# Two of every four blocks of attention probabilities turned by VectorE and a round trip through DRAM, with keys stored in strips

## The chip, the cores and the metric

The kernel runs on one NeuronCore of a Trainium2 chip. The number that counts is the device time of one execution in microseconds. The kernel before took 1162.42 us (median of three runs, 1162.05 to 1164.58). The core has a matrix engine (TensorE; PE in the profile, with PEld for the loads of its stationary operand), a vector engine (VectorE; DVE), an activation engine (ScalarE; ACT), GpSimd (POOL) and SyncE (SP), whose queue issues every DMA of this kernel. All data are float32.

## The reference, cut to what matters

```python
x = x + layernorm(attention(layernorm(x)))   # x: 4 sequences of 512 tokens, 1024 wide
x = x + layernorm(ffn(layernorm(x)))

# attention: 32 query heads of width 32, 8 key/value heads, rotary positions
scores = einsum('bhqd,bhkd->bhqk', q, k) / sqrt(32)
scores = where(causal, scores, -1e20)
attn   = softmax(scores, axis=-1)
out    = einsum('bhqk,bhkd->bhqd', attn, v)  # then @ w_o.T + b_o

# ffn: x @ base_w.T + base_b + 2 * LoRA mixture of the 2 best of 8 experts
```

Softmax runs over the keys. The product with v sums over keys too, so on TensorE the keys of the probabilities must lie on the partitions, while the scores come out with the queries on the partitions. The probabilities therefore have to be transposed between the two.

## The kernel before, in words

**Tiles.** The 2048 tokens are 16 tiles of 128, four to a sequence; tile i of a sequence (i = 0 to 3) attends to i + 1 key blocks of 128. The dense products (q, w_o and the base matrix of the ffn) are done for pairs of token tiles with a seven-product scheme (`seven`, L655). Each of their weight blocks, a "piece" of 128 x 512 (256 KB), is read from DRAM for one use, through a ring of `RING` = 13 buffers (`bring_pieces`, L476; issue at L489). The products are issued at L618. The key and value weights stay in SBUF.

**A group.** Attention goes by groups (`Group`, L1371). A group is one token tile and n = 4, 2, 1, 1 columns of heads for i = 0, 1, 2, 3; a column holds four heads, one in each 32-partition strip, and these four are the "quadrants" r. A group has m = n (i + 1) = 4, 4, 3, 4 key blocks in each quadrant. `scores` (L1382) issues the score products into the one PSUM tile `sc`; VectorE adds the causal mask and takes the maxima (L1459, L1469); ScalarE takes the exponentials into a tile `pr` for each quadrant and sums them (L1411); VectorE inverts the sums (L1440); GpSimd multiplies `pr` by them (L1425). `turn` (L1480), once for each quadrant, transposes the m blocks of `pr` on TensorE (L1485) into a PSUM bank, which is copied to a tile `prT` (`copy`, L331, on ScalarE or VectorE). `values` (L1498) then issues the products with v (L1508), and its result is copied to `aT`, the input of the w_o product. `pr` and `prT` share the `SOFT` = 8 buffers of one pool.

**The order of the work** is not left to the engines. `Order` (L92) runs through the whole program in advance with written durations, and emits each engine's instructions in the order that results; an engine then executes its own list strictly in that order and waits where data are not there. Some of its durations: a DMA occupies SP's queue for its kilobytes divided by `RATE` = 370 and is taken to have landed `LANDS` = 2.8 us later; a dense product takes 0.858 us; a hand-over between engines 0.1 us (`SIGNAL`).

TensorE's steps stand in lanes: scores; urgent transposes of activations; a value lane, which holds in turn the four turns of a group, its values step, the turns of the next group, and so on; and the dense lanes. `_choice` (L202) takes the first lane in that order that has been ready for `SAFE` = 0.3 us. A values step is put last while the next scores step "comes", that is while everything the scores need apart from the exponentials before them has been planned; and in the kernel before a scores step is put last while the values step comes but is not ready. If the values step is ready when scores are issued, both go out together (`tensor`, L236), with one switch of TensorE into its 32-row or 32-column tiling. The scores of group k also need the turns of group k - 2.

**SP.** Every DMA stands in SP's one list: pieces, x tiles (`load_x`, `load_y`), results, and in the first 240 us the sums and differences of weight blocks that the seven-product scheme needs, which `mix` (L409) computes and writes to DRAM. A DMA that has to wait for a semaphore keeps everything behind it in the list waiting.

Of the kernel before, what the change touches and what calls it, by code (L numbers as in the profile page):

```python
# [16 lines left out]
P = 128  # L17
# [5 lines left out]
MASKED = -1e30  # L23
QUADS = P // HD


# [65 lines left out]
class Order:  # L92
# [109 lines left out]
    def _choice(self, scores, values, lanes):  # L202
# [7 lines left out]
        if score is not None and value is not None:  # L210
            if self._comes(score):
                waiting.append(values)
            if self._comes(value) and not self._is_ready(value):
                waiting.append(scores)
        for lane in lanes:
# [50 lines left out]
def kernel(  # L266
# [26 lines left out]
    QSCALE = 1.0 / math.sqrt(HD)  # L293
    BANKS, SOFT, RING = 4, 8, 13

# [5 lines left out]
    kvpool = ctx.enter_context(tc.tile_pool(name="kvpool", bufs=4))  # L301
    soft = ctx.enter_context(tc.tile_pool(name="soft", bufs=SOFT))
    weights = ctx.enter_context(tc.tile_pool(name="weights", bufs=RING))
    small = ctx.enter_context(tc.tile_pool(name="small", bufs=2))
# [6 lines left out]
    banks = Slots(BANKS)  # L311
    soft_slots, part_slots, piece_slots = Slots(SOFT), Slots(4), Slots(RING)
    xnT_slots, aT_slots, hT_slots = Slots(2), Slots(3), Slots(2)
    qT_slots, kT_slots, raw_slots, turn_slots = Slots(8), Slots(4), Slots(6), Slots(1)
    xa_slots, y_slots, w_slots, v_slots = Slots(1), Slots(3), Slots(4), Slots(8)
    order = Order(banks)
# [14 lines left out]
    def copy(n, out, in_):  # L331

        return Op(
            0,
            act=(0.15 + n * 0.00085, lambda: nc.scalar.copy(out(), in_())),  # L335
            dve=(0.15 + n * 0.00105, lambda: nc.vector.tensor_copy(out(), in_())),  # L336
        )
# [9 lines left out]


    ident = const.tile([P, P], F32, name="ident")
    make_identity(nc, ident)  # L350
    cmask = const.tile([P, P], F32, name="cmask")
    make_causal_mask(nc, cmask, MASKED)

# [141 lines left out]
    class Norm:  # L495
# [60 lines left out]
        def apply(self, dst, src, h):  # L556
            cols = slice(h * 512, (h + 1) * 512)
            yield Op(
                self.urgent,
                dve=(  # L560
                    0.66,
                    lambda: nc.vector.tensor_scalar(
                        dst()[:, cols], src()[:, cols], self.rstd, self.shift, ALU.mult, ALU.add
                    ),
                ),
                act=(
                    0.82,
                    lambda: nc.scalar.activation(  # L568
                        dst()[:, cols], src()[:, cols], AF.Identity, bias=self.shift, scale=self.rstd
                    ),  # L570
                ),
            )
# [299 lines left out]
    def load_y(tok):  # L872

        yield y_slots.take()
        yield has_rest if tok in pairs[0] else all_mixed

        def issue():
            tok.y = xpool.tile([P, D], F32, tag="y", bufs=3, name=f"y_{tok.t}")
            nc.sync.dma_start(out=tok.y, in_=x[tok.t * P : (tok.t + 1) * P, :])

        yield sp(P * D * 4 / 1024 / RATE, issue)
        yield LANDS
        tok.has_y.finish(order.at)
# [33 lines left out]
    def keys_values(job):  # L917
# [38 lines left out]
        def turn_k():  # L956
# [4 lines left out]
            def end():  # L961
                yield step_k.done
                raw_slots.give(order.at)
                for kt in range(NKT):
                    yield copy(
                        P,
                        lambda: seq.k_tile(kt)[:, i * P : (i + 1) * P],
                        lambda: pt[:, kt, :],
                    )
# [401 lines left out]
    class Group:  # L1371
        def __init__(self, tok, at, n):
# [6 lines left out]
            self.pr, self.prT = [None] * QUADS, [None] * QUADS  # L1379
            self.has_prT = [Task() for _ in range(QUADS)]  # L1380

    def scores(g):  # L1382
# [19 lines left out]
        def quadrant(r):  # L1402
            urgent = 1 + r / QUADS
            yield soft_slots.take()
            pr = soft.tile([P, GROUP, P], F32, tag="soft", name=f"pr_{g.name}_{r}")
            pr = g.pr[r] = pr.rearrange("p a b -> p (a b)")
            for c in range(g.n):
# [3 lines left out]
                    lambda: nc.scalar.activation(  # L1411
                        pr[:, c * n : (c + 1) * n],
                        sc4[:, r, c, :],
                        AF.Exp,
# [6 lines left out]
            for c in range(g.n):  # L1421
# [3 lines left out]
                    lambda: nc.gpsimd.tensor_scalar(  # L1425
                        pr[:, c * n : (c + 1) * n],
                        pr[:, c * n : (c + 1) * n],
                        rtot[:, r, c : c + 1],
# [48 lines left out]
        for h in range(QUADS // 2):  # L1477
            start(totals(h), order.now)

    def turn(g, r):  # L1480
# [17 lines left out]
    def values(g):  # L1498
# [5 lines left out]
        for c in range(g.n):  # L1504
            for j in range(i + 1):
                for r in range(QUADS):
# [3 lines left out]
                        lhsT=g.seq.v[j][:, head * HD : (head + 1) * HD],  # L1510
                        rhs=g.prT[r][:, c * (i + 1) + j, :],
                        start=(j == 0),
# [3 lines left out]
        def end():  # L1516
            yield g.valued.done
            for r in range(QUADS):
                soft_slots.give(order.at)
            yield copy(  # L1520
                g.n * P, lambda: tok.aT[:, g.at : g.at + g.n, :], lambda: av[:, : g.n, :]
# [84 lines left out]
    for k, g in enumerate(groups):  # L1606
# [4 lines left out]
        if k > 1:  # L1611
# [4 lines left out]
            Step(0.109 * blocks, partial(turn, g, r), [g.normed[r | 1]], bank=True, turns=True)  # L1616
            for r in range(QUADS)
        ]
# [135 lines left out]
```

## Time and profile before

| | before |
|---|---|
| median of three runs | 1162.42 us |
| profiled execution: its time, its span | 1164.45 us, 1162.7 us |
| mean granted TensorE clock | 0.996 |
| DVE, ACT, POOL busy | 832.6, 530.1, 611.7 us |
| DMA queue of SP: bytes, busy share of 16 DMA engines | 230.12 MB, 60.7% |
| transposes of probabilities on PE (L1485) | 1280, weight loads 144.5 us busy |
| copies of `prT` on ACT, on DVE | 261 for 134.1 us, 91 for 58.3 us |
| normalisation of `pr` on POOL (L1425) | 512 for 300.5 us |

A row of the profile's groups gives the line, the engine, the operation, output and inputs, their shapes, how often it ran, the busy time and the mean duration, and what the engine waited for. A dense product and a score product each appear as two records. PE records overlap, so PE's time for a step is better read from the distance of one start to the next than from the durations. The queue of SP is written SPq.

### The profile page before, as it was taken

What the parts mean: (1) busy time and instruction counts of PE and PEld (TensorE: products, weight loads), DVE (VectorE), ACT (ScalarE), POOL (GpSimd) and SP (SyncE); (2) the same over time, 40 slices, a digit from 0 to 9 for tenths busy, and PEclk for the clock granted to TensorE, in tenths of its full rate; (3) what the DMA queues carried; (4) which work ended last, traced back from release to release, by engine and by line L of the source; (5) the groups of instructions that cost most, each with busy time, mean ns of one, the idle gap of its engine ahead of it and who ended that gap; (6) DMA issues with size and microseconds to landing.
All of it is one profiled execution on the core that took longest, in us unless ns stands there. A gap on an engine that the chain in (4) does not pass through costs nothing.

```text
span 1162.7 us, 21371 instructions
## 1 busy us (share of the span) xinstructions
PE 1136.4 (98%) x7240; PEld 624.5 (54%) x7240; DVE 832.6 (72%) x1629; ACT 530.1 (46%) x1545; POOL 611.7 (53%) x859
## 2 busy tenths in 40 slices
PE   7999999999999999999999999999999999999997
PEld 3455554655556455565555555456555555556443
DVE  4787767987678756787667876768866787668564
ACT  0354554555555355555434434455644555454010
POOL 2686856743756435544555253654545564547231
PEclk9999999999999999999999999999999999999999
DMA  9879777563773637625477443673457745585783
GB/s 349 277 255 310 248 253 263 170 220 97 257 239 96 199 109 253 192 83 176 141 244 256 137 135 118 219 229 106 149 168 233 243 135 160 164 268 187 221 285 118
DMA packets 117740, 231.48 MB, mean 199 GB/s; under 512 B 13440, under 2 KB 14464, under 8 KB 117632
## 3 DMA queue, kind: packets, MB, share of 16 engines
q1 hardware_dynamic: 117632, 230.12, 60.7%
q8 instruction: 58, 0.95, 0.3%
q14 instruction: 50, 0.41, 0.1%
HBM read 209.09 MB, written 20.97 MB: 198 GB/s over the span
## 4 chain that ended last, share of the span: by engine, by line
PE 86%; DVE 7%; DMA 3%; POOL 1%; ACT 1%; issue 1%; SPq 0%; POOLq 0%; ACTq 0%
PE acc_f L618 18%; PE acc_o L618 16%; PE acc_q L618 14%; PE pt_p L1485 11%; PE acc_kv L618 8%; PE sc L1390 7%; PE av L1508 6%; PE acc_gl L618 2%; DVE nmax L1469 2%; PE pt_xn L593 1%; PE pt_h L593 1%; DMA piece<-in_w_qkv_dram 1%; ACT pr L1411 1%; PE pt_q L1010 1%; DMA xa<-in_x_dram 1%
## 5 line engine op out<-in xcount | busy, mean ns | idle before, releaser
L1425 POOL TENSOR_SCALAR pr<-pr,rtot 128x256 f32<-128x256 f32 (+3 forms) x512 | 300.5, 602 | 251.9 <-DVE rtot L1440 183.3
L1411 ACT ACTIVATE pr<-sc,nmax 128x256 f32<-128x256 f32 (+3 forms) x512 | 265.0, 536 | 121.8 <-DVE nmax L1469 63.6
L1469 DVE TENSOR_REDUCE nmax<-sc 128x2 f32<-128x768 f32 (+3 forms) x176 | 198.2, 1126 | 33.7 <-ACT pr L1411 30.6
L1485 PEld LDWEIGHTS pt_p<-ident,pr 128*128 128x128 f32 x1280 | 144.5, 141 | 59.3 <-issue 49.1
L1485 PE MATMUL pt_p<-ident,pr 128*128 128x128 f32 x1280 | 173.2, 276 | 2.4 <-DVE raw_q L727 1.0
L335 ACT COPY prT<-pt_p 128x512 f32<-128x512 f32 (+1 forms) x261 | 134.1, 548 | 62.4 <-PE pt_p L1485 61.0
L1459 DVE TENSOR_TENSOR sc<-sc,cmask 128x256 f32<-128x256 f32 (+2 forms) x176 | 96.7, 550 | 48.6 <-PE sc L1390 39.0
L335 ACT COPY aT<-av 128x128 f32<-128x128 f32 (+2 forms) x83 | 26.1, 315 | 222.1 <-PE av L1508 222.0
L618 PE MATMUL acc_f<-piece,s_f 128*128 128x512 f32 x256 | 120.1, 602 | 2.1 <-DVE s_f L343 2.1
L618 PE MATMUL acc_kv<-wkv_sb,T_xn 128*128 128x512 f32 x256 | 119.4, 597 | 0.0
L1411 ACT ACTIVATION_READ_ACCUMULATOR pr<-sc,nmax 128x1 f32 x512 | 108.3, 212 | 0.0
L618 PE MATMUL acc_o<-piece,aT 128*128 128x512 f32 x232 | 105.9, 594 | 0.0
L618 PE MATMUL acc_q<-piece,s_q 128*128 128x512 f32 x224 | 105.4, 595 | 0.1
L618 PE MATMUL acc_q<-piece,T_xn 128*128 128x512 f32 x224 | 103.9, 594 | 0.1
L618 PE MATMUL acc_o<-piece,s_o 128*128 128x512 f32 x224 | 102.8, 593 | 0.0
L1390 PE MATMUL sc<-kT,qT 32*128 32x384 f32 (+3 forms) x1024 | 93.9, 464 | 0.5 <-ACT pr L1411 0.5
L1508 PEld LDWEIGHTS av<-prT,v 128*32 128x32 f32 x2560 | 64.8, 109 | 50.1 <-issue 35.0
L618 PE MATMUL acc_f<-piece,T_h 128*128 128x512 f32 x192 | 90.0, 592 | 0.0
L343 POOL TENSOR_TENSOR y<-y,w 128x512 f32<-128x512 f32 x61 | 79.1, 1309 | 20.3 <-ACT w L568 14.9
L1508 PE MATMUL av<-prT,v 128*32 128x128 f32 x2560 | 88.7, 276 | 0.2 <-DVE prT L336 0.2
L336 DVE COPY prT<-pt_p 128x512 f32<-128x512 f32 (+1 forms) x91 | 58.3, 642 | 31.3 <-PE pt_p L1485 29.7
L541 POOL TENSOR_TENSOR rstd<-veps,neg_half 128x1 f32<-128x1 f32 x64 | 35.0, 549 | 86.1 <-DVE veps L537 85.8
(154 smaller groups left out, 1416.3 us busy)
## 6 DMA issues: line engine op xcount, KB each, us to landing
piece<-mixed_f SPq DMA_DIRECT2D x128, 256.0 KB, 3.5
piece<-in_w_o_dram SPq DMA_DIRECT2D x116, 256.0 KB, 3.6
piece<-mixed_q SPq DMA_DIRECT2D x112, 256.0 KB, 3.4
piece<-mixed_o SPq DMA_DIRECT2D x112, 256.0 KB, 4.1
piece<-in_w_qkv_dram SPq DMA_DIRECT2D x100, 256.0 KB, 3.7
piece<-in_w_base_dram SPq DMA_DIRECT2D x96, 256.0 KB, 3.3
xa<-in_x_dram SPq DMA_DIRECT2D x32, 256.0 KB, 3.8
y<-in_x_dram SPq DMA_DIRECT2D x16, 512.0 KB, 5.7
```

Source lines behind the costliest of these rows:

```text
L335: act=(0.15 + n * 0.00085, lambda: nc.scalar.copy(out(), in_())),
L336: dve=(0.15 + n * 0.00105, lambda: nc.vector.tensor_copy(out(), in_())),
L343: engine.tensor_tensor(out=out(), in0=in0(), in1=in1(), op=op)
L541: nc.gpsimd.tensor_tensor(out=self.rstd, in0=self.veps, in1=neg_half, op=ALU.pow)
L618: nc.tensor.matmul(acc[0][:, :n], lhsT=lhsT(c), rhs=w(c), start=(c == 0), stop=last)
L1390: nc.tensor.matmul(sc[:, r, c * n : (c + 1) * n], lhsT=tok.qT[g.kt][rows, (g.at + c) % GROUP, :], rhs=seq.kT[g.kt][rows, :n], start=True, ...
L1411: lambda: nc.scalar.activation(pr[:, c * n : (c + 1) * n], sc4[:, r, c, :], AF.Exp, bias=nmax[:, r, c : c + 1], accum_out=total[:, r, c : ...
L1425: lambda: nc.gpsimd.tensor_scalar(pr[:, c * n : (c + 1) * n], pr[:, c * n : (c + 1) * n], rtot[:, r, c : c + 1], 1.0, ALU.mult, ALU.mult,),
L1459: lambda: nc.vector.tensor_tensor(out=diag, in0=diag, in1=cmask.unsqueeze(1).unsqueeze(1).to_broadcast([P, q, g.n, P]), op=ALU.add,),
L1469: lambda: nc.vector.tensor_reduce(nmax[:, some, : g.n], sc4[:, some], AX.X, ALU.max, negate=True),
L1485: nc.tensor.transpose(pt[:, j, :], g.pr[r][:, j * P : (j + 1) * P], ident)
L1508: nc.tensor.matmul(av[r * HD : (r + 1) * HD, c, :], lhsT=g.seq.v[j][:, head * HD : (head + 1) * HD], rhs=g.prT[r][:, c * (i + 1) + j, :], ...
```

## The change

Quadrants 0 and 1 of each group (r < `TURNED` = 2) are turned as before. Quadrants 2 and 3 go another way, in the new function `flip`: VectorE transposes each 32 x 32 square of the two quadrants' probabilities in place with one instruction (1024 elements a partition where m = 4, 768 where m = 3); a DMA writes the tile to a DRAM tile `there`; a second DMA, which waits for the first to land, reads it back into a tile `flat`, with rows placed so that the whole blocks come out transposed. The first moves 4 KB runs (3 KB where m = 3), the second 1 KB runs (768 B). The values products read `flat` in four runs of 32 elements.

For this the keys inside each block of 128 are held in another order: the copies to `kT` and the causal mask put key 4k + s at place 32s + k. The exponentials of quadrants 0 and 1 are written back in the original order (steps of four elements); those of quadrants 2 and 3 go into the tile `pair`, by strips.

Room and order change with it: `pair` and `flat` have two buffers each of 4 KB a partition; `SOFT` goes from 8 to 7, `RING` from 13 to 8, the y tiles from three to two. `copy` and `Norm.apply` run on ScalarE alone, where they could also go to VectorE. `_choice` no longer puts a scores step last while the values step is not ready. `Order` plans the rest around this.

```diff
-            if self._comes(value) and not self._is_ready(value):
-                waiting.append(scores)
...
-    BANKS, SOFT, RING = 4, 8, 13
+    BANKS, SOFT, RING = 4, 7, 8
+    PAIRS, FLATS = 2, 2
+    SIDE = 32
+    NS = P // SIDE
...
-    xa_slots, y_slots, w_slots, v_slots = Slots(1), Slots(3), Slots(4), Slots(8)
+    xa_slots, y_slots, w_slots, v_slots = Slots(1), Slots(2), Slots(4), Slots(8)
...
             act=(0.15 + n * 0.00085, lambda: nc.scalar.copy(out(), in_())),
-            dve=(0.15 + n * 0.00105, lambda: nc.vector.tensor_copy(out(), in_())),
...
+    def strips_of(a):
+        return a.rearrange("p (s k) -> p s k", s=NS)
+    def by_strip(a):
+        return a.rearrange("p (k s) -> p s k", s=NS)
...
-                        lambda: seq.k_tile(kt)[:, i * P : (i + 1) * P],
-                        lambda: pt[:, kt, :],
+                        lambda: strips_of(seq.k_tile(kt)[:, i * P : (i + 1) * P]),
+                        lambda: by_strip(pt[:, kt, :]),
...
+    def flip(g):
+        m = g.n * (g.tok.i + 1)
+        q = QUADS - TURNED
+        yield pair_slots.take()
+        g.pair = flips.tile([P, NS, q, m, SIDE], F32, tag="pair", bufs=PAIRS, name=f"pair_{g.name}")
+        g.has_pair.finish(order.at)
+        yield g.normed[TURNED:]
+        flat_pair = g.pair.rearrange("p s r m k -> p (s r m k)")
+        yield dve(
+            0.1 + NS * q * m * SIDE * 0.00105,
+            1,
+            lambda: nc.vector.transpose(out=flat_pair, in_=flat_pair),
+        )
+        there = dram.tile([NS, P, q * m * SIDE], F32, tag="there", bufs=4, name=f"there_{g.name}")
+        us = P * NS * q * m * SIDE * 4 / 1024 / RATE
+        yield sp(us, lambda: nc.sync.dma_start(
+            out=there.rearrange("a (k s) r -> (a k) (s r)", s=NS), in_=flat_pair), -1)
+        yield LANDS
+        pair_slots.give(order.at)
+        yield flat_slots.take()
+        g.flat = flips.tile([P, NS, q, m, SIDE], F32, tag="flat", bufs=FLATS, name=f"flat_{g.name}")
+        yield sp(us, lambda: nc.sync.dma_start(
+            out=g.flat.rearrange("p a r m q -> p a (r m q)"), in_=there.rearrange("a p r -> p a r")), -1)
+        yield LANDS
+        for r in range(TURNED, QUADS):
+            g.has_prT[r].finish(order.at)
...
-                        rhs=g.prT[r][:, c * (i + 1) + j, :],
+                        rhs=(
+                            g.prT[r][:, c * (i + 1) + j, :]
+                            if r < TURNED
+                            else g.flat[:, :, r - TURNED, c * (i + 1) + j, :]
+                        ),
...
             Step(0.109 * blocks, partial(turn, g, r), [g.normed[r | 1]], bank=True, turns=True)
-            for r in range(QUADS)
+            for r in range(TURNED)
```

## The prediction

> **What bounds the kernel now.** I read the page's busy time first, then the chain that ended last.
>
> ```profile
> PE 1136.4 (98%) x7240; PEld 624.5 (54%) x7240; DVE 832.6 (72%) x1629; ACT 530.1 (46%) x1545; POOL 611.7 (53%) x859
> ...
> PE 86%; DVE 7%; DMA 3%; POOL 1%; ACT 1%; issue 1%; SPq 0%; POOLq 0%; ACTq 0%
> PE acc_f L618 18%; PE acc_o L618 16%; PE acc_q L618 14%; PE pt_p L1485 11%; PE acc_kv L618 8%; PE sc L1390 7%; PE av L1508 6%; PE acc_gl L618 2%; DVE nmax L1469 2%; PE pt_xn L593 1%; PE pt_h L593 1%; DMA piece<-in_w_qkv_dram 1%; ACT pr L1411 1%; PE pt_q L1010 1%; DMA xa<-in_x_dram 1%
> ```
>
> TensorE is the bound: 86% of the chain is its work, and the list of waits gives PE itself some 18 us in all, 7.3 of them before its first instruction. So work taken from PE is worth its full length only while nothing new makes PE wait. The transposes are 11% of the chain.
>
> Next I read the order of time in a stretch of i = 3 (start, duration, engine; the bracket is idle time).
>
> ```profile
> 449.79 0.31 PEld L1390 LDWEIGHTS sc<-kT,qT 32*128 32x128 f32 x8 [0.76 <-issue]
> 449.79 1.14 PE L1390 MATMUL sc<-kT,qT 32*128 32x512 f32 x8
> 450.86 0.86 PE L1508 MATMUL av<-prT,v 128*32 128x128 f32 x24
> ...
> 457.03 3.12 POOL L1425 TENSOR_SCALAR pr<-pr,rtot 128x512 f32<-128x512 f32 x4 [3.06 <-DVE rtot L1440]
> ...
> 459.13 1.14 PE L1390 MATMUL sc<-kT,qT 32*128 32x512 f32 x8
> ...
> 460.20 0.86 PE L1508 MATMUL av<-prT,v 128*32 128x128 f32 x24
> 460.99 1.09 PE L1485 MATMUL pt_p<-ident,pr 128*128 128x128 f32 x8
> ```
>
> Groups follow each other every 9.1 to 9.3 us (sc at 440.67, 449.79, 459.13). A group's probabilities are normalised 10.4 us after its scores began (457.03 + 3.12 = 460.15). Each values step (av) leaves directly behind scores of a later group, so it waits for its partner and has slack.
>
> Last, the DMA rows (KB each, median us from issue to landing) and SP's own waits.
>
> ```profile
> piece<-mixed_q SPq DMA_DIRECT2D x112, 256.0 KB, 3.4
> y<-in_x_dram SPq DMA_DIRECT2D x16, 512.0 KB, 5.7
> mixed_q<-mix_q SPq DMA_DIRECT2D x8, 512.0 KB, 7.3
> mixed_f<-mix_f SPq DMA_DIRECT2D x8, 512.0 KB, 4.4
> ...
> SPq L489 <- DMA mixed_q<-mix_q: 27.3, 4, 7.5
> ```
>
> A 512 KB transfer lands after 4.4 to 7.3 us. The last line: four times SP stood before a piece because that piece reads what an earlier DMA was still writing, up to 7.5 us, with all other DMAs behind it.
>
> **The change, part by part.** The sum is made on the span, 1162.7 us; the profiled run took 1164.45, the median is 1162.42, so a span counts as a time here.
>
> *Transposes removed.* 640 of 1280. 11.3% of the chain for 1280 is 131.4 us, 0.103 each (8 from 460.99 take 0.82 us to the next load: the same). **-65.7 us.**
>
> *Pairing lost.* Scores entered with 0.76 us idle on the weight loader against the usual 0.24: 0.52 us for the switch of tiling; av behind them adds about 0.2. A values step that goes alone pays 0.52 in place of 0.2. By the argument below about two in three of 88 groups (176 reductions at L1469, two a group) go alone: 59 x 0.32 = **+19 us**; 0 to 28.
>
> *The new way to `flat`.* 56 groups have 512 KB in each direction, 32 have 384 KB: 41.9 MB out and 41.9 MB back. The plan gives it, after normalising: VectorE 1.18 + 0.1, then twice 1.38 on SP + 0.1 + 2.8, 9.8 us in all, so values at 10.4 + 9.8 = 20.2 us after the scores. Two periods are 18.5, so scores k+2 have gone, and scores k+3 do not "come", because they need the turns of k+1, which stand behind values k in the lane. So values k are planned the moment that they are ready, plus 0.3 (SAFE) and half a dense step (0.43): 0.7 us of slack. On the chip: 1.22 (nearest VectorE row, the 1024-element maximum) + 5.7 + 5.7 (the y row) = 12.6 us, 2.8 later than planned. PE executes in the planned order and waits, and behind values k stand the turns, the next scores and all dense work. Between scores k and values k lie the waits of three values steps, so each is (2.8 - 0.7)/3 = 0.7 us: 88 x 0.7 = **+62 us**. Bounds: nothing if the plan leaves 2.1 us more; with 7.3 out and 7.1 back (wgl, 544 KB in 544 B runs), (5.8 - 0.7)/3 x 88 = 150. I take y because its load state is that of most of the run.
>
> Here a rule speaks for the change: the Trainium skill, "DMA: Bandwidth & Descriptors", section "Anatomy of one DMA", fits 2.0 us + bytes/436 GB/s to a transfer (by the GpSimd path), 3.2 us for 512 KB. By it both legs take 6.4 us, less than the planned 8.6, and this term is zero: 1148 us in all. The rows of this trace say 4.4 to 7.3, so I keep the row.
>
> *SP's list.* The first leg waits for VectorE, the second for the first to land; behind both stand pieces, x tiles and results. The second leg is planned 4.3 us after the first and lands at 5.7: SP is blocked 1.4 us a group. What hid a late piece was the ring: 13 x 0.86 = 11.2 us of dense work, now 8 x 0.86 = 6.9, less 3.5 to land: 3.4 us. One block fits, one together with a y tile and two legs in the queue does not. Between 0 and 1.4 us a group; I take 0.25, near the end where the ring covers it: **+22 us**; upper bound 123.
>
> *The first 200 us.* Shares of the DMA engines in 29 us windows there: 0.97, 0.82, 0.73, 0.92, 0.72, 0.79, 0.79, with 15 groups (30 maxima). About 15 MB more at 400 GB/s, which the best short slices reached, is 38 us; idle is 18% of 203 = 36 us. It just fills: 0 to 40, I take **+10 us**.
>
> *What I cost at nothing.* VectorE loses copies (91.1 us) and normalisations (38.7) and gains 56 x 1.22 + 32 x 0.96 = 99 us. ScalarE: 530 - 134 (`prT` now) + 97 (176 copies at 0.587 or 0.482) + 29 (other copies) + 47 (58 at 0.811) = 569 us, 49%: hidden by PE, but every copy out of PSUM now queues behind exponentials, which come 4 in 3.6 us, and four banks wait for it. Strided forms have no row: exponentials of quadrants 0 and 1, GpSimd's multiply by strips, `kT`, values reading four runs. From 0 to twice their time, the first two would add up to 1.5 us a group to the chain to `flat`, the last up to 36 us to PE; I take 0, the row of the plain form. `SOFT` 7 and two y tiles: at most 6 probability tiles are held at once; 0.
>
> **Sum:** 1162.7 - 65.7 + 19 + 62 + 22 + 10 = **1210 us**.
>
> A rule against the change: "TensorE: Matmul & The Clock Gate", section "The HAM clock gate", halves PE's clock after an idle window of about 3.4 us. This trace shows it already near the end (PE busy, its loads, the others; then clock, DMA share, GB/s):
>
> ```profile
> 1128.77 5.40 PE L618 MATMUL acc_f<-piece,s_f 128*128 128x512 f32 x8 [2.10 <-DVE s_f L343]
> ...
> 1130.00:1132.00 2.00, 2.00 (x4) 0.81 (x3) 1.69 (x10) 0.00 (x0) 0.13 (x1) 0.55 0.40 130
> 1132.00:1134.00 2.00, 2.00 (x4) 0.73 (x3) 0.19 (x1) 0.00 (x0) 0.00 (x0) 0.60 0.57 145
> ```
>
> 2.1 us of idle brought the clock to 0.55, and 8 records took 5.2 us in place of 3.4: a wait of 2 us costs nearly 4. By the rule alone waits of 0.7 us are free of it, by the row waits from about 2 us are not; so the sum has none, and the upper case has it.
>
> **Rivals.** (1) *The transit is covered, and it gets faster.* Two quadrants need only be there by values; if the plan holds values k for the scores of k+2 or k+3, 2.1 us more are free and only pairing, SP and start remain: 1162.7 - 65.7 + 19 + 10 = 1126, down to 1107 if pairs stay. It decides as long as values wait under 0.5 us a group (47/88). For it: no wait of PE today, and periods of 13 us on average (1162/88). Against: 9.2 us where i is 2 or 3, and 5.7 us for 512 KB. Chance 0.18. (2) *DMA becomes the bound.* 230 MB keep the engines busy 706 us; 84 MB more at the same 326 GB/s add 257, with short runs at half speed in the second leg up to 400: 963 to 1110 us, and windows that stand at 0.78 with three groups would need 1.1 to 1.3. Legs then land after 7 to 9 us, pieces miss the ring of 8, PE waits over 2 us and its clock falls: 1.5 us a group at SP in place of 0.25 gives 1320; I give it 1250 to 1340. Against: slices of 400 GB/s exist. Chance 0.23. (3) *Gain and waits cancel* within 0.2% (2.3 us, about what a measurement of this kernel can tell): 0.03.
>
> **How the numbers follow.** The likeliest case, waits for `flat` larger than the transposes saved, has 0.56, and a range of its own of 1165 to 1250. The range 1125 to 1300 leaves out the deeper part of (1) and the upper part of (2), about 0.09 each. Faster is (1), 0.18; same 0.03; slower 0.79.
>
> **What would show it.** The trace after should have 640 transposes; waits of PE or PEld at L1508 for DMA `flat` of 40 to 100 us; SPq waiting for DMA `there` in most groups; legs landing at 5 to 7 us; waits for pieces above today's 3 us a line; av mostly not directly behind sc. I am wrong if values wait for nothing (then rival 1), or if waits for pieces exceed those for `flat` (rival 2).

## The result, and the profile after

The changed kernel took **1221.62 us** (median, 1218.12 to 1224.64), beside 1163.12 us for the kernel before on the same chip: a ratio of **1.050**, 95% interval 1.047 to 1.053. The profiled execution took 1221.72 us, its span is 1220.0, 57.3 more than before.

The page's busy times, the granted clock in 40 slices, and the DMA queue's row:

```profile
PE 1118.3 (92%) x6600; PEld 568.3 (47%) x6600; DVE 804.3 (66%) x1491; ACT 600.0 (49%) x1581; POOL 627.0 (51%) x874
...
PEclk9998889999899999999999999999999999989969
...
q1 hardware_dynamic: 176768, 314.01, 76.2%
```

The 640 transposes are gone (6600 records for 7240), yet PE is busy only 18.1 us less, and it idles 101.7 us (1220.0 - 1118.3) where it idled 26.3. The clock row shows one cause: it dips in the slices from 91 to 183 us, at 305 us and near the end; the mean is 0.971, before 0.996.

The page's groups that answer to the change's parts (busy, mean ns of one, idle before):

```profile
L1432 ACT ACTIVATE pr<-sc,nmax 128x128 f32<-128x128 f32 (+3 forms) x256 | 202.9, 844 | 265.8 <-DVE sc L1480 143.2
...
L1570 PE MATMUL av<-flat,v 128*32 128x128 f32 x1280 | 90.5, 283 | 23.6 <-DMA flat<-there 23.5
...
L1547 PE MATMUL pt_p<-ident,pr 128*128 128x128 f32 x640 | 99.6, 291 | 12.2 <-ACT aT L340 7.7
L1432 ACT ACTIVATE pair<-sc,nmax 128x128 f32<-128x128 f32 (+3 forms) x256 | 133.5, 541 | 2.8 <-issue 1.8
L1515 DVE STREAM_TRANSPOSE pair<-pair 128x1024 f32<-128x1024 f32 (+1 forms) x88 | 100.2, 1139 | 10.4 <-POOL pair L1446 10.1
...
L1570 PE MATMUL av<-prT,v 128*32 128x128 f32 x1280 | 93.5, 282 | 0.3 <-DVE w L733 0.3
```

Values that read `flat` in four runs take 283 ns, those that read `prT` 282: the strided read is free. Exponentials that are written back in the original order (`pr`) take 844 ns in the mean, those written by strips (`pair`) 541: that form is not.

The DMA rows (KB each, median us from issue to landing), then two rows of PE's waits and three of SP's (us in all, times, longest):

```profile
piece<-mixed_f SPq DMA_DIRECT2D x128, 256.0 KB, 4.3
...
there<-pair SPq DMA_DIRECT2D x56, 512.0 KB, 3.7
piece<-mixed_q SPq DMA_DIRECT2D x112, 256.0 KB, 4.4
flat<-there SPq DMA_DIRECT2D x56, 512.0 KB, 4.9
```

```profile
PE av L1570 <- DMA flat<-there: 23.5, 14, 4.9
PE pt_h L599 <- ACT w L574: 13.8, 2, 10.1
```

```profile
SPq L1522 <- DVE pair L1515: 123.0, 57, 7.4
SPq L1533 <- DMA there<-pair: 102.3, 69, 5.1
...
SPq L885 <- DMA out_dram<-y: 15.6, 12, 2.4
```

The two transfers land after 3.7 and 4.9 us, together 8.6, just what the plan gives them (2 x 4.3). PE waits for `flat` only 14 times (its weight loads 20 times, for 28.9 us). SP stands 102 us before second transfers and 123 us before first ones that wait for their squares. Pieces land after 4.4 us where it was 3.4 (`mixed_q`).

The long `pt_h` wait is in the last tiles. The timeline there (start, duration, engine; the bracket is idle time):

```profile
1169.38 0.45 SPq L1308 DMA_DIRECT2D out_dram<-y  x1
...
1173.49 0.33 SPq L885 DMA_DIRECT2D y<-in_x_dram  x1
...
1177.18 1.26 POOL L347 TENSOR_TENSOR y<-y,w 128x512 f32<-128x512 f32 x1 [3.85 <-DMA y<-in_x_dram]
...
1182.63 1.97 PE L599 MATMUL pt_h<-ident,w 128*128 128x128 f32 x8 [10.14 <-ACT w L574]
```

A y tile is loaded only after the result of an earlier token tile has been stored out of the same buffer; the sum, the norm and PE's transposes stand behind it, and PE idles 10 us.

**Where the 57 us lie.** PE idle: +75.4. PE busy: -18.1.

Of the added idle time, 23.5 us are waits for `flat` and 13 the longer waits at `pt_h`. The other 39 are many short ones, mostly for ScalarE and VectorE: 7.7 us at `pt_p` for the copies to `aT` (none before), 15.6 before the transposes of keys and queries (4.2 before), 5.7 at scores for the exponentials into `pair` (0.5 before).

The busy time holds three parts. The 640 transposes at 0.103 us are -65.7. The switches into a 32-wide tiling rise from 102 to 163 in PE's timeline; a stretch of the changed kernel shows what one costs:

```profile
123.82 5.31 PE L624 MATMUL acc_q<-piece,s_q 128*128 128x512 f32 x12
129.06 0.93 PE L1398 MATMUL sc<-kT,qT 32*128 32x384 f32 x8
129.92 1.99 PE L624 MATMUL acc_q<-piece,s_q 128*128 128x512 f32 x4
131.74 1.88 PE L624 MATMUL acc_q<-piece,T_xn 128*128 128x512 f32 x4
133.55 0.30 PE L1570 MATMUL av<-prT,v 128*32 128x128 f32 x2
```

Dense records start 0.43 us apart. The twelve before the scores take 5.24 us, 0.09 more than 12 x 0.43; the four behind them 1.82, 0.10 more; the four before the values step again 0.09 more. Two steps that go out together enter and leave the tiling once in place of twice, so 61 more switches are about +12 us (61 x 0.2).

The clock is the third part. The granted clock is 0.50 in 70 us of the changed kernel, and PE is busy in 48.6 of them (3.4 before). Half of the difference is +23 us; the mean clock, 1220 x 0.029 less 1162.7 x 0.004, gives 31, of which 8 fall where PE has nothing to do. The three parts give -31. Of the 13 us that are missing, some 9 can be the ends of records before a wait, by estimate: PE waits 76 times in place of 20, and a dense record lasts 0.59 us where the next one would start after 0.43. The rest is unexplained.

**A second reading, of the written order.** `Order` writes the lists with its own durations, so the kernel's code, with `Order` run by itself, also says when it believes that SP's last instruction ends. That is no measurement, but it splits a measured difference into what was already in the lists and what the chip added. Before: planned end 1159.2 us with 20.3 us of planned idle on PE, measured span 1162.7. After: planned 1148.1 with 71.8 idle, measured 1220.0. **The lists promise a kernel 11 us faster; the chip takes 72 us more than they say.** The order pays 51.5 us of added idle out of 62.6 us of PE work saved. Beyond the plan are 68.4 us more than before: 24 of idle (101.7 - 71.8 less 26.3 - 20.3) and 44 of busy time, in which the clock has its 23.

### The profile page after: what moved, and what is told of

Its sections match the earlier page's. It is cut to its first block, busy times and chain, and to the rows that moved or that the text cites. A ratio compares the mean times of both kernels' runs of the same rounds, so it can differ in the third digit from the quotient of the medians.

```text
span 1220.0 us, 20077 instructions
## 1 busy us (share of the span) xinstructions
PE 1118.3 (92%) x6600; PEld 568.3 (47%) x6600; DVE 804.3 (66%) x1491; ACT 600.0 (49%) x1581; POOL 627.0 (51%) x874
## 3 DMA queue, kind: packets, MB, share of 16 engines
q1 hardware_dynamic: 176768, 314.01, 76.2%
## 5 line engine op out<-in xcount | busy, mean ns | idle before, releaser
L1432 ACT ACTIVATE pr<-sc,nmax 128x128 f32<-128x128 f32 (+3 forms) x256 | 202.9, 844 | 265.8 <-DVE sc L1480 143.2
L1446 POOL TENSOR_SCALAR pr<-pr,rtot 128x128 f32<-128x128 f32 (+3 forms) x256 | 153.0, 611 | 262.5 <-DVE rtot L1461 192.8
L1446 POOL TENSOR_SCALAR pair<-pair,rtot 128x128 f32<-128x128 f32 (+3 forms) x256 | 149.5, 597 | 9.5 <-DVE rtot L1461 8.8
L1432 ACT ACTIVATE pair<-sc,nmax 128x128 f32<-128x128 f32 (+3 forms) x256 | 133.5, 541 | 2.8 <-issue 1.8
L624 PE MATMUL acc_o<-piece,aT 128*128 128x512 f32 x232 | 111.7, 618 | 0.5 <-ACT aT L340 0.4
L1570 PE MATMUL av<-flat,v 128*32 128x128 f32 x1280 | 90.5, 283 | 23.6 <-DMA flat<-there 23.5
L1547 PE MATMUL pt_p<-ident,pr 128*128 128x128 f32 x640 | 99.6, 291 | 12.2 <-ACT aT L340 7.7
L1515 DVE STREAM_TRANSPOSE pair<-pair 128x1024 f32<-128x1024 f32 (+1 forms) x88 | 100.2, 1139 | 10.4 <-POOL pair L1446 10.1
L340 ACT COPY prT<-pt_p 128x512 f32<-128x512 f32 (+1 forms) x176 | 91.9, 557 | 23.0 <-PE pt_p L1547 22.3
L1547 PEld LDWEIGHTS pt_p<-ident,pr 128*128 128x128 f32 x640 | 73.3, 146 | 47.1 <-issue 28.8
```

The lines of the kernel that those rows point to most:

```text
L624: nc.tensor.matmul(acc[0][:, :n], lhsT=lhsT(c), rhs=w(c), start=(c == 0), stop=last)
L1432: lambda: nc.scalar.activation(exp_out[c], exp_in[c], AF.Exp, bias=nmax[:, r, c : c + 1], accum_out=total[:, r, c : c + 1],),
L1446: lambda: nc.gpsimd.tensor_scalar(to[c], to[c], rtot[:, r, c : c + 1], 1.0, ALU.mult, ALU.mult,),
L1515: lambda: nc.vector.transpose(out=flat_pair, in_=flat_pair),
L1547: nc.tensor.transpose(pt[:, j, :], g.pr[r][:, j * P : (j + 1) * P], ident)
L1570: nc.tensor.matmul(av[r * HD : (r + 1) * HD, c, :], lhsT=g.seq.v[j][:, head * HD : (head + 1) * HD], rhs=(g.prT[r][:, c * (i + 1) + j, :] ...
```

## The experiments

Two theories stood first: values wait for `flat`, as the prediction has it; or the room given up (y tiles, ring, `SOFT`) and the strided exponentials cost more than the waits for `flat`. The texts quoted under the experiments have theories of their own, with letters; H stands for two different ones, in experiments 10 and 12. Each measured median is followed by its ratio to the kernel before with the interval.

**1. Two y tiles, in the kernel before.**

```diff
-    xa_slots, y_slots, w_slots, v_slots = Slots(1), Slots(3), Slots(4), Slots(8)
+    xa_slots, y_slots, w_slots, v_slots = Slots(1), Slots(2), Slots(4), Slots(8)
...
-            tok.y = xpool.tile([P, D], F32, tag="y", bufs=3, name=f"y_{tok.t}")
+            tok.y = xpool.tile([P, D], F32, tag="y", bufs=2, name=f"y_{tok.t}")
```

> The kernel before with two y tiles in place of three, nothing else. Theory A (the end of the changed kernel is late because the third y tile is gone: the last tile's x can only be read once a result that used its buffer is stored): 18 to 30 us slower than before, with a wait of PE at pt_h near the end and a y load behind out_dram. Theory B (the late end comes from the round trip through DRAM): within 3 us of before.

1177.62 us, 1.0127 [1.0109, 1.0145]. PE's longest wait, and the chain before it in the timeline:

```profile
PE pt_h L593 <- DVE w L562: 12.0, 3, 8.2
```

```profile
1125.93 0.38 SPq L1302 DMA_DIRECT2D out_dram<-y  x1
1129.75 0.37 SPq L879 DMA_DIRECT2D y<-in_x_dram  x1
...
1139.34 1.94 PE L593 MATMUL pt_h<-ident,w 128*128 128x128 f32 x8 [8.21 <-DVE w L562]
```

14 us, fewer than the 18 to 30 expected, by the chain seen above at the end of the changed kernel. With three y tiles the last y load is issued at 1111.12 us, here at 1129.75, behind the stores of 1122 and 1126 us. SP's waits before y loads are not longer in all (10.8 us, 12.7 before); the last one comes later. The lists have it too: their planned end moves from 1159.2 to 1175.8, the span from 1162.7 to 1176.2.

**2. Keys in natural order.** The keys, the mask and quadrants 0 and 1 go plain, and the exponentials of quadrants 2 and 3 read the scores in steps of four instead. The order of the instructions is the same, but for one copy of the mask.

```diff
-                        lambda: strips_of(seq.k_tile(kt)[:, i * P : (i + 1) * P]),
-                        lambda: by_strip(pt[:, kt, :]),
+                        lambda: seq.k_tile(kt)[:, i * P : (i + 1) * P],
+                        lambda: pt[:, kt, :],
...
-                exp_out = [a.rearrange("p (j k s) -> p j s k", s=NS, k=SIDE) for a in to]
+                exp_out = to
...
+                exp_in = [a.rearrange("p (j k s) -> p j s k", s=NS, k=SIDE) for a in exp_in]
```

> The changed kernel with keys, mask and the exponentials of quadrants 0 and 1 in their natural order (no write in steps of four); only the exponentials of quadrants 2 and 3 read the scores in steps of four. Theory C (the strided write makes ScalarE late, then VectorE's squares and SP's list): mean of the exponentials of quadrants 0 and 1 back near 0.54 from 0.84 us, SP's wait for the squares under 60 of 123 us, 15 to 40 us faster than the changed kernel. Theory D (the two legs' landing times make the waits): exponentials shorter, but no more than 5 us faster, and waits for flat stay above 20 us. If a read in steps of four costs as much as the write, the exponentials of quadrants 2 and 3 go to 0.84 and the time stays.

1201.45 us, 1.033 [1.0307, 1.0352]: 20 us less than the changed kernel. ScalarE's groups by form, the changed kernel first, then this one:

```profile
L1432 ACT ACTIVATE pr<-sc,nmax 128x512 f32<-128x512 f32 x64 | 75.4, 1198 | 78.2 <-DVE nmax L1490 40.5 <-DVE sc L1480 34.5 <-PE acc_q L624 2.6
...
L1432 ACT ACTIVATE pair<-sc,nmax 128x512 f32<-128x512 f32 x64 | 43.7, 690 | 1.8 <-issue 1.8
```

```profile
L1430 ACT ACTIVATE pr<-sc,nmax 128x512 f32<-128x512 f32 x64 | 43.9, 688 | 75.6 <-DVE nmax L1488 37.3 <-DVE sc L1478 33.8 <-PE acc_f L623 4.1
L1430 ACT ACTIVATE pair<-sc,nmax 128x512 f32<-128x512 f32 x64 | 43.7, 689 | 1.8 <-issue 1.8
```

1198 ns fall to 688, while the strided read of the scores leaves 689 where it was 690. The planned end is the same (1148.1), so these 20 us are all the chip's. Theory C has the time but only part of the path: SP's waits for the squares fall from 123.0 to 96.6 us, not under 60, and PE's waits for `flat` stay (24.7). What shrinks is PE's waiting for ScalarE, at `pt_p` for `aT` from 7.7 to 2.9 us and at scores for `pair` from 5.7 to 1.9.

**3. The order told of the longer exponentials**, in the changed kernel.

```diff
-                    0.5 + n * 0.00079,
+                    0.5 + n * (0.00179 if r < TURNED else 0.00079),
```

> The changed kernel, with only the duration that the order of work assumes for the exponentials of quadrants 0 and 1 raised from 0.5 + 0.00079 n to 0.5 + 0.00179 n, as measured. If the waits come from an order made for shorter exponentials (part of theory C): 5 to 20 us faster, waits of PE for flat under 10 of 23.5 us. If they come from the legs (theory D) or from the longer exponentials themselves: within 5 us.

1234.62 us, 1.0603 [1.0584, 1.0623]: slower by 13, which neither theory of the quoted text has. PE still waits 23.6 us for `flat`. The planned end moves by 35.6 us, to 1183.7, of which the chip gives back 22.7: a true duration makes the order plan idle time that the chip then keeps.

**4. Three y tiles, paid with two probability tiles.**

```diff
-    BANKS, SOFT, RING = 4, 7, 8
+    BANKS, SOFT, RING = 4, 5, 8
...
-    xa_slots, y_slots, w_slots, v_slots = Slots(1), Slots(2), Slots(4), Slots(8)
+    xa_slots, y_slots, w_slots, v_slots = Slots(1), Slots(3), Slots(4), Slots(8)
```

> The changed kernel with three y tiles again; the 4 KB come from the pool of probabilities, 5 tiles in place of 7. Theory A: 18 to 30 us faster than the changed kernel, and no wait of PE at pt_h of 10 us near the end; the smaller pool may give some of it back in the middle. Theory B: no more than 5 us faster, or slower.

1211.7 us, 1.0415 [1.0399, 1.043]: 10 us less, where 18 to 30 or at most 5 were expected. No wait for `pt_h` is near 10 us any more; waits of scores for ScalarE have taken some of its place (15.8 us), while those for `flat` are down to 14.8. The y tile has its price here as well, less what `SOFT` 5 costs.

**5. Natural keys, everything turned on TensorE.** This is experiment 2 without the squares and the two transfers; ring 8, two y tiles, copies on ScalarE alone and the new choice stay. `SOFT` is 8, and the buffers of the rotary step (`raw`) are five for six, so the room is not quite that of experiment 2.

```diff
-            if r < TURNED:
+            if r < g.on_pe:
...
+        g.on_pe = QUADS
...
-    BANKS, SOFT, RING = 4, 7, 8
+    BANKS, SOFT, RING = 4, 8, 8
```

> The kernel of after_natural in which no group takes the way through DRAM: all four quadrants are turned on TensorE again, but rings (8 pieces, two y tiles), copies on ScalarE alone and the changed choice of scores stay (8 probability tiles and 5 raw tiles, to hold four quadrants). What it loses against the kernel before is the price of room and order alone. Theory E (room and order cost more than the round trip): 1190 us or more, so that the flips themselves gain. Theory D (the round trip costs): 1178 to 1185 us, the y tile's 14 us and a few more, and the flips lose some 20 us against it.

1185.16 us, 1.0188 [1.0163, 1.0213]. So the room and the order cost 22 us in all (14 the y tile), as the lists have it (planned end 1180.6 for 1159.2), and the round trip itself a net 16 (1201.45 - 1185.16). Values go out with scores again here (102 switches), so the net holds the lost pairs too.

**6. Only the first 22 groups on TensorE**, a sequence's worth.

```diff
+        g.on_pe = QUADS if k < 22 else TURNED
```

> The kernel of after_natural in which the 22 groups of the first sequence (until some 240 us, while mix still reads and writes weights) turn all four quadrants on TensorE, the other 66 two (8 probability tiles and 5 raw tiles). Theory F (the way through DRAM is bad only beside the DMAs of the start): the 22 groups give back 16 us of transposes saved, but the start's loss of some 30 us goes: 10 to 25 us faster than after_natural, PE waits for flat under 14 of 24.7 us. If the start is slow for another reason (room, ScalarE's copies): 5 to 20 us slower than after_natural.

1203.93 us, 1.0338 [1.0319, 1.0358], beside 1201.45: 2.5 us slower, in neither expected range. That the crowded start is the main cost falls.

**7. The transfers planned 1 and 2 us later**, as they land, with natural keys.

```diff
-        yield LANDS
+        yield 3.8
         pair_slots.give(order.at)
...
-        yield LANDS
+        yield 4.8
         for r in range(TURNED, QUADS):
```

> The kernel of after_natural in which the order of work assumes the first leg to land 1 us later and the second 2 us later than before (3.8 and 4.8 in place of 2.8 us after the issue), so that values are planned 3 us later. Theory D: the waits of PE for flat (24.7 us) fall under 10 us and the time by 10 to 25 us. If dense work put between does not cover it (the lane or the banks run out): waits move to other lines and the time stays within 5 us.

1220.06 us, 1.0476 [1.0459, 1.0494]: 19 us slower, again a miss of both theories. The two rows of PE's waits that show why:

```profile
PE sc L1397 <- ACT pair L1430: 17.0, 5, 5.0
PE av L1568 <- DMA flat<-there: 14.3, 6, 5.1
```

The waits for `flat` fall from 24.7 to 14.3 us, and scores wait in their place. The planned end moves from 1148.1 to 1193.9.

**8. Copies and normalisations free to go to VectorE again**, with natural keys.

```diff
+            dve=(0.15 + n * 0.00105, lambda: nc.vector.tensor_copy(out(), in_())),
```

> The kernel of after_natural with copies out of PSUM and the normalisations of Norm on VectorE or ScalarE again, whichever is free in the order. Theory G (copies queued behind exponentials on ScalarE are the loss): 10 to 25 us faster than after_natural, fewer waits of PE for aT, prT and kT copies. If ScalarE's 49% hid them, as the prediction has it: within 5 us, or slower because VectorE's squares come later.

1221.1 us, 1.0483 [1.0447, 1.0519]: 20 us slower. The plan itself is 29.2 us later (1177.3 for 1148.1). So theory G falls: VectorE's help does not pay in the order that comes of it. That ScalarE alone costs nothing is not shown by this.

**9. The old choice restored** (scores last while values come but are not ready), with natural keys.

```diff
+            if self._comes(value) and not self._is_ready(value):
+                waiting.append(scores)
```

> The kernel of after_natural with the choice of the kernel before: scores are put last again while the next values step is not ready, so that the two go out together. If the 61 more switches of TensorE into its tiling are worth 20 us and nothing else is lost: 10 to 20 us faster than after_natural, with switches back from 163 towards 102. If the scores that now wait for flat set the pace of the groups: slower by 20 us or more.

1253.91 us, 1.0758 [1.0736, 1.0781]: 52 us slower. Pairs return (72 of 88 values steps directly behind scores, 13 without it; switches 103 for 163), and scores pay:

```profile
PE av L1570 <- DMA flat<-there: 28.5, 15, 4.6
...
PE sc L1399 <- ACT pair L1432: 21.7, 11, 6.1
```

**10. No transfers.** Natural keys, squares on VectorE, and values read the squares straight from `pair`. Left out are the two transfers, so the probabilities of quadrants 2 and 3 are turned only inside their squares.

```diff
-        yield sp(us, lambda: nc.sync.dma_start(
-            out=there.rearrange("a (k s) r -> (a k) (s r)", s=NS), in_=flat_pair), -1)
...
-        yield sp(us, lambda: nc.sync.dma_start(
-            out=g.flat.rearrange("p a r m q -> p a (r m q)"), in_=there.rearrange("a p r -> p a r")), -1)
+        g.flat = g.pair
```

> The kernel of after_natural without the two DMAs of the round trip: values read the tile of squares as VectorE left it (so the blocks are not fully transposed and the attention of quadrants 2 and 3 is not the reference's); four tiles of squares in place of two and two. Theory D in its wider form (the two legs, by landing, by SP's list or by load, make what the flips lose): the 66 us of transposes less 20 us of switches show, 1135 to 1155 us, and PE waits little at av. Theory H (the loss lies in the order itself, with squares and values off the usual rhythm): 1175 us or more.

1142.25 us, 0.9806 [0.9788, 0.9823]. The transfers cost 59 us, and turning half the blocks by squares alone gains 43 (1185.16 - 1142.25). The pairs of scores and values come back as well (68 of 88, 106 switches for 163), so some 11 of the 59 us are switches (57 x 0.2). The page's clock row and queue row, then SP's longest waits:

```profile
PEclk9999999989999999999999999999999999999969
...
q1 hardware_dynamic: 117632, 230.12, 61.5%
```

```profile
SPq L500 <- PE acc_q L623: 243.9, 194, 19.5
SPq L500 <- PE acc_f L623: 240.5, 202, 14.6
```

Of the early dips of the clock one slice is left. SP waits mostly for PE to free a ring buffer: it is ahead.

**11. The transfers as a mere load.** Experiment 5, with squares and both transfers run beside it and not used. They keep their places in the plan and in SP's list; the squares read `pr`, whose tile comes free only after them.

```diff
+        start(flip(g), order.now)
```

> The kernel of natural_no_flips with the squares and both legs running beside it for every group, read by nobody (two square instructions of 512 elements a group): the load without the dependency. If the load is what costs (DMA engines, SP's list with the ring of 8, VectorE's 100 us): 30 us or more above natural_no_flips' 1185, with waits of PE for pieces. If what costs is values waiting for flat: within 10 us of 1185.

1233.05 us, 1.058 [1.0565, 1.0596]: nobody waits for `flat`, and the load costs 48 us all the same. The waits of PE for pieces that the quoted text expects hardly come (7.7 us in all, 1.9 in experiment 5).

**12. The same, and the second transfer reads a DRAM tile that was written once**, so that it never waits for the first.

```diff
-                out=g.flat.rearrange("p a r m q -> p a (r m q)"), in_=there.rearrange("a p r -> p a r")
+                out=g.flat.rearrange("p a r m q -> p a (r m q)"), in_=kept[m].rearrange("a p r -> p a r")
```

> The kernel with all turns on TensorE and the squares and both transfers run beside it unused (1233 us), with one change: the second transfer of a group reads a DRAM tile that was written once at the start, so it has the same bytes and runs but never waits for the first transfer of its group. As there, what the transfers bring isn't used; the output is complete. Theory H, that the wait in SP's list is the cost: SP's 140 us of waiting for there vanishes, the pieces come in time, and most of the 48 us goes back: 1190 to 1205 us. Theory I, that the 84 MB on the DMA engines are the cost: the pieces still land about 1 us later than without the transfers, and the time stays at 1225 to 1235 us. Half of each would give about 1212.

1229.33 us, 1.0553 [1.0533, 1.0574]. SP's waits in 11, then in 12:

```profile
SPq L1537 <- DMA there<-pair: 140.3, 72, 6.2
SPq L500 <- PE acc_q L623: 112.0, 139, 8.0
```

```profile
SPq L500 <- PE acc_q L623: 143.2, 150, 7.7
...
SPq L1542 <- DMA kept<-pair: 5.0, 2, 4.2
```

With SP's 140 us of waiting for the first transfer brought to 5, **only 4 of the 48 come back** (the two intervals overlap): theory H falls, and theory I has the time. But this does not show that the bytes are the cost. SP stands almost as long as before, for other things: before pieces, mostly for PE to free a ring buffer (510 us in all for 447), and before the first transfers (181 for 151). And the planned order is the same in both. Theory I named later pieces too, and they land 0.6 to 1.1 us later than in experiment 5 (`mixed_f` 3.2 us there, `mixed_o` 4.4 there and 5.5 here). Two DMA rows of 12:

```profile
piece<-mixed_f SPq DMA_DIRECT2D x128, 256.0 KB, 3.8
...
flat<-kept SPq DMA_DIRECT2D x56, 512.0 KB, 5.9
```

Yet PE's waits for pieces are 6.5 us in all (7.7 in experiment 11), so late pieces are no large part of it either. Of the two theories of the start, the second has 14 us for the y tile and 20 for the strided form; the first has 23.5 us of waits for `flat`, and experiments 10 to 12 say that the transfers cost far more than these. The lists give a part of the answer.

**The planned ends beside the spans** (us; the plan is what the kernel's own order computes, the spans are measured):

| kernel | planned idle of PE | planned end | span | span less plan |
|---|---|---|---|---|
| before | 20.3 | 1159.2 | 1162.7 | 3.5 |
| 1 two y tiles | 36.9 | 1175.8 | 1176.2 | 0.4 |
| after | 71.8 | 1148.1 | 1220.0 | 71.9 |
| 2 natural keys | 71.8 | 1148.1 | 1202.9 | 54.8 |
| 3 told | 107.4 | 1183.7 | 1232.9 | 49.2 |
| 4 three y tiles, `SOFT` 5 | 82.5 | 1157.5 | 1209.1 | 51.6 |
| 5 all on TensorE | 41.1 | 1180.6 | 1184.0 | 3.4 |
| 6 first 22 on TensorE | 67.1 | 1159.3 | 1202.7 | 43.4 |
| 7 planned later | 117.0 | 1193.9 | 1224.3 | 30.4 |
| 8 VectorE free to copy | 101.3 | 1177.3 | 1217.3 | 40.0 |
| 9 old choice | 141.4 | 1209.7 | 1252.6 | 42.9 |
| 10 no transfers | 57.4 | 1125.8 | 1136.7 | 10.9 |
| 11 load only | 69.2 | 1209.9 | 1232.5 | 22.6 |
| 12 load, no wait at SP | 69.2 | 1209.9 | 1228.2 | 18.3 |

Three things stand in it. Kernels without the transfers run as planned, within 11 us; all with them are 18 to 72 us late. Of the 48.5 us by which the load lengthens the span (11 less 5), 29.3 are in the lists before anything runs, since the transfers have planned times on SP and buffers to wait for, and 19.2 are the chip's. And of the 66.2 us between experiments 2 and 10, 22.3 are planned and 43.9 are the chip's, so more than half of what the transfers cost comes on the chip, where the order believed it away. (By the medians the 66.2 are 59.2, and 36.9 the chip's: experiment 10 was profiled in its fastest execution, experiment 2 in its slowest.)

PE's own record says what kind of time this is. The load of experiment 11 adds 30.9 us of idle time to PE, and the plan has 28.1 of them; it adds 17.6 us of busy time, of which some 10 are the halved clock. Between experiments 2 and 10 PE's idle time differs by 29.2 us (14.4 planned) and its busy time by 37.0, of which some 12 are the clock and 11 the switches; the rest is not assigned.

How the chip adds it shows in one stretch. PE busy (records), the other engines, then the granted clock, the DMA share and GB/s; first experiment 2, then 5:

```profile
120.00:180.00 60.00, 47.59 (x301) 24.62 (x301) 42.93 (x75) 27.35 (x83) 43.09 (x48) 0.89 0.78 273
```

```profile
120.00:180.00 60.00, 59.41 (x412) 32.49 (x404) 48.36 (x84) 33.37 (x97) 38.43 (x43) 1.00 0.78 264
```

With the same DMA share PE idles 12.4 us in place of 0.6, and the mean clock is 0.89 in place of 1.00. So a high DMA share alone does not lower the clock.

## Why the prediction was right

The sign was right, and the time (1210) lay 12 us under the measured 1222, inside the likeliest case's own range. That the sum came so near is luck in good part: the terms for `flat`, SP's list and pairing were too large, and what was put at nothing (y tile, strided exponentials, clock, planned idle time) made up for them.

| step of the sum | said | what the runs show |
|---|---|---|
| Transposes removed | -65.7 | 640 gone; PE busy is 63.1 less in experiment 10 than in 5: held |
| Pairing lost | +19 | 75 of 88 go alone, where 14 did: 61 more (59 foreseen), but at some 0.2 us, not 0.32: +12. The 0.32 was read from idle time of the weight loader, most of which lies beside PE's work |
| The new way to `flat` | +62 | PE waits 23.5 us for `flat` |
| SP's list | +22 | its mechanism, blocking by the second transfer, is worth 4 us at most between experiments 11 and 12 |
| The first 200 us | +10 | not measured apart: experiment 6 takes the transfers out of the first 22 groups and moves the time by 2.5. How late the scores are is no measure: behind 256 score records the changed kernel is 14.1 us late (295.2 for 281.1), experiment 5 without any transfer 15.4 |
| Two y tiles | 0 | 14 in the kernel before |
| Strided exponentials | 0 | 20 |
| Clock | none | 31 by its mean, 23 of them while PE works |

**The step that failed in mechanism is "the new way to `flat`".** It took the y row, 5.7 us, for both transfers, and so 2.8 us of lateness at every group. They landed in 3.7 and 4.9, together the 8.6 that the plan has (twice 1.38 + 0.1 + 2.8), so most values steps had nothing to wait for. The estimate of 3.2 us by the Trainium skill's fit ("DMA: Bandwidth & Descriptors", section "Anatomy of one DMA") lay below both and the chosen row above both; the `mixed_f` row of 4.4 us, which stood in the same fence, is near their mean of 4.3. With landings as measured the sum's own formula gives nothing for `flat`, and 1148 us. What stood in the place of the 62 us is the waits of 23.5, the two costs put at nothing, the clock, and idle time that the order itself plans: the prediction treated the plan as having none of its own, where it has 51.5 us more than before. That could have been worked out from the kernel's own durations, and not from the trace of before.

**Two costs were wrongly put at nothing.** For the y tiles the text counted probability tiles and never followed the y buffer: the load waits for a store, and at the end of the run nothing hides it. The cover that it should have named was the dense work of other pairs, which the last pair does not have. For the strided forms "from 0 to twice" held the answer (1198 for 690 ns is 1.74 times), and the choice of 0 was the error; the other forms, GpSimd's multiply by strips (597 and 611 ns), values in four runs and the strided read of the scores, cost no more than their plain forms. ScalarE alone for copies, also put at nothing, was not measured apart: it is within the 7 to 8 us that experiment 5 leaves beside the y tile, and with the longer exponentials PE did wait for such copies (experiment 2).

**The clock was weighed and then left out.** The text had it that waits from 2 us slow PE and put that in the upper case. The row of before was a good guide. In the changed kernel each of PE's ten waits of 2.1 us and more comes with 3.4 to 13.7 us at a granted clock of 0.50, from within the wait or just behind it; of the 23 waits from 0.7 to 1.8 us one does by itself (1.1 us at 288.5 us, close behind two shorter ones). Four of the ten are for `flat` (3.7, 4.9, 2.1 and 3.9 us), the others for ScalarE and VectorE. The rule of the Trainium skill ("TensorE: Matmul & The Clock Gate", section "The HAM clock gate"), a halved clock after an idle window of about 3.4 us, would allow it only for the longer of these; here waits of 2.1, 2.9 and 3.1 us did it as well. Two windows early in the changed kernel and one around the 10 us wait show it; the mean falls from 0.996 to 0.971:

```profile
122.00:152.50 30.50, 24.52 (x172) 13.18 (x170) 21.91 (x38) 15.15 (x44) 24.13 (x27) 0.89 0.87 311
152.50:183.00 30.50, 23.32 (x128) 11.23 (x127) 20.37 (x36) 14.74 (x39) 19.08 (x22) 0.83 0.63 217
1159.00:1189.50 30.50, 16.29 (x61) 11.99 (x62) 10.89 (x35) 9.18 (x15) 9.52 (x13) 0.66 0.26 84
```

The windows' columns are as in the stretch above: 0.89, 0.83 and 0.66 are the granted clock of the changed kernel.

**Of the signs named in advance**, 640 transposes, SP waiting for `there` in most groups (69 times) and values mostly not behind scores came; waits of 40 to 100 us for `flat`, landings at 5 to 7 us and pieces above 3 us a line did not. Rival 2, DMA as the bound, has the queue's share at 76.2% and later pieces for it; against it are waits of PE for pieces of at most 2.2 us a line, and the second transfer, which did not run at half speed (4.9 us for 3.7). Rival 1 lacked the other half of its condition: values seldom wait, but the kernel is slower all the same. Its 1126 also leaves out the 22 us of SP's list that its text counts among what remains.

The parts in order: y tile 14, the rest of room and order 7 to 8, the round trip net 16 (59 of transfers less 43 of transposes), strided exponentials 20: 57 to 58 of the 58.5 us. They add up because each is the difference of two neighbouring kernels, so the sum is no proof of them, and in another order the parts could differ.

**What stays open.** How the 48 us of the load divide between the transfers' places in the lists, VectorE's squares, which run beside copies there, and the DMA engines' share is known only as planned (29) and not planned (19). No run has the same bytes without their places in the plan. The ring of 8 was not made larger beside the transfers, for want of room. A version with three y tiles, natural keys and the transfers was not run.

## What to carry to other kernels

When the order of work is written out with assumed durations, ask first how much idle time the new order plans and then how far the chip can keep it: here a change that the plan had 11 us faster came out 57 us slower, and giving the plan truer durations made it slower still. Follow every buffer that is given up to the end of the run, where no other work hides its reload. And where a rearrangement must cost a stride somewhere, try it on the side that reads PSUM before the side that writes SBUF: for the exponentials here the one was free and the other was not.

## What the runs showed of the hardware that was not expected

- ScalarE's exponential written in steps of four float32 takes 1198 ns for 512 elements and 956 for 384, where plain it takes 688 and 581: about 1 ns more an element. Read from PSUM in steps of four it costs nothing (689 and 581).
- VectorE's transpose of 32 x 32 squares in place, 88 times, took 1139 ns in the mean, 1236 for 1024 elements a partition and 969 for 768; so the row chosen for it, a maximum over as many elements (1.22 us), was right within 0.02 us.
- A 512 KB write to DRAM of 4 KB runs landed in 3.7 us, its reading back in 1 KB runs in 4.9, while 256 KB pieces went from 3.4 to 4.4 us (`mixed_q`).
- Removing a wait of 140 us in SP's queue, with all bytes kept, moved the time by 4 us.
- Entering the 32-wide tiling held PE up by 0.09 us, leaving it behind scores by 0.10.
- In the kernel before and the changed one every wait of PE from 2.1 us on, behind its first instruction, came with a granted clock of 0.50 for 3.4 us or more; waits up to 1.8 us, but for one, did not.
